# Attention outputs stored as 64 rows and one row, keys stored once and loaded in two pieces

## The chip, the core and the metric

The kernel runs on one core of a Trainium2 chip. The metric is device microseconds of one execution; three executions of the kernel before took 1837.16, 1839.26 and 1840.21 us, and their median, 1839.26 us, is the time before. One more execution was taken with the hardware profiler; all views below are of that one.

A core has a matrix engine (TensorE, PE in the profile; PEld is its weight load), a vector engine (DVE), a scalar engine (ACT), a general engine (POOL) and SyncE (SP), which computes nothing and here issues almost all DMAs. Each engine works through its own list of instructions in order. A DMA is issued by one engine's queue ("SPq" in the views) and then carried out by 16 DMA engines that all queues share.

## The reference, cut to what matters

One layer of gated cross-attention and a gated feed-forward, in float32, on 16 x 128 = 2048 tokens of width 1024:

```python
# x: (16, 128, 1024); ctx_4096: (16, 128, 1024)
def xattn(queries, keys, values, Wq, Wk, Wv, Wo):    # 32 heads of 32, 8 key/value heads, groups of 4
    q = (queries @ Wq).reshape(b, s, KV_HEADS, GROUP, HEAD_DIM)
    k = (keys @ Wk).reshape(b, s, KV_HEADS, HEAD_DIM)
    v = (values @ Wv).reshape(b, s, KV_HEADS, HEAD_DIM)
    scores = jnp.einsum('bqhgd,bkhd->bhgqk', q, k) * scale
    attn = jax.nn.softmax(scores, axis=-1)
    return jnp.einsum('bhgqk,bkhd->bqhgd', attn, v).reshape(b, s, EMBED) @ Wo
def ffn(x, W_gate, W_up, W_down):                     # width 2752
    return silu(x @ W_gate.T) * (x @ W_up.T) @ W_down.T
x = x + jnp.tanh(g_xattn[0]) * xattn(_layernorm(x), ctx_4096, ctx_4096, Wq, Wk, Wv, Wo)
x = x + jnp.tanh(g_ffn[0]) * ffn(_layernorm(x), W_gate, W_up, W_down)
```

Each of the 16 sequences has 128 tokens and attends only to its own 128 context rows, so attention falls into 16 x 8 = 128 independent pieces of 128 keys by 4 x 128 queries.

## The kernel before

**Numbers in two parts.** The matrix engine multiplies in a shortened float32. Every operand is therefore split into a high part (the rounded number) and a low part (the rest), by `split`: a copy on ACT and a subtraction on DVE. A product is three matmuls: high x high, high x low, low x high (`mm3`).

**Stages.** Tokens are handled in two halves of 1024 (`NGRP`), with blocks of 512 (`TB`). `projections` makes keys, values and queries for both halves and sends them to DRAM: `kd`, `vd`, `qd`. `attention` reads them back, piece by piece, and sends outputs to `od`. `outer` reads `od`, multiplies by the output projection, adds the residual and normalizes; `run` then does the feed-forward, with seven products in place of eight.

**Attention is woven into other work.** It is a generator; the host loop takes one step of it at a time between its own matmuls. The first half's attention (called stage 1 here) runs inside the second half's projections, from about 107 to 348 us; the second half's (stage 2) runs inside the feed-forward of the first half, from about 478 to 861 us. The instruction order on each engine is the order in which the Python code issues the work; nothing rearranges it. What DMAs SP issues therefore stand in one list: loads of attention, stores of attention, loads and stores of the host.

**One cell of attention** is one sequence and two key/value heads, so 64 cells, 32 in each stage, and two units in each cell. For a cell, SP issues `vta` (values, L458), `ks` (keys, L451) and `qs` in two pieces (L465, L466). The keys of a cell lie in SBUF on 96 partitions: high part, high part again, low part, 32 rows each, so that one matmul over 96 rows does the three products at once with the queries' high, low, high. For that `kd` holds three parts: `evacuate` (L246 to L255) stores high and low with one DMA into its parts 1 and 2, and the high part with a second DMA into part 0; one DMA (L451) then loads the 96 rows. `ks` has two buffers, and its next load is issued once the second score matmul of its cell is done.

A unit goes through `scores` (PE, L472), `take` (ACT copy, then a maximum over partitions on POOL, L483), `shift` (DVE, L486), `expo` (ACT, L489 and L491), `rest` (DVE, L495), `gather` (PE, L500 and L501) and `leave` (a copy of 80 rows out of PSUM into `os`, L511, on ACT, or in stage 1 in turn on ACT and DVE). Values are padded with 16 columns of ones (`ONES`), so that `gather` gives 64 rows of outputs (with the values' high part and low part) and 16 equal rows that hold the sums of the softmax. `leave` stores all 80 rows to `od` with one DMA (L515). In stage 1 the store is issued a step later, and `os` has three buffers; in stage 2 it is issued at once, and `os` has one buffer, so that the next copy has to wait for the store to land. When a sequence's eight units are stored, the row of sums (row 64, one of the sixteen) is fetched as `rc` (L526), inverted, and kept in `rd`. `outer` reads rows 0 to 31 and 32 to 63 of `od` and the inverted sums of `rd`.

**Semaphores of DMAs.** SP's DMAs take eight semaphores in turn; a DMA is issued only when the one eight before it has landed.

## Time and profile before

| | |
|---|---|
| median of three executions | 1839.26 us (1837.16 to 1840.21) |
| profiled execution | 1839.81 us, span of its instructions 1838.0 us |
| PE | busy 1816.5 us, 99% of the span, 8296 matmuls |
| DVE, ACT, POOL | busy 1210.6, 900.7 and 546.3 us |
| DMA | 373.55 MB in 232565 packets, mean 203 GB/s |
| `od<-os` | 128 DMAs of 160 KB, median 4.0 us from issue to landing |
| `ks<-kd` | 64 DMAs of 96 KB, 4.0 us |
| `kd<-e` | 8 DMAs of 512 KB, 6.7 us, and 8 of 256 KB, 6.8 us |
| `rd<-rc` | 16 DMAs of 16 KB, 2.4 us |

Busy time is the union of an engine's instructions. An entry of the view of waits says which engine stood idle before which instruction, who ended the wait, and for how long in total, how often and at longest. A line `SPq L515 DMA_DIRECT2D od<-os` of the timeline is the issuing of a DMA, with start and duration; the transfer itself goes on after that, until its landing. The chain of waits is followed back from the last instruction: at each step to what released it. "PEclk" is the matrix engine's granted clock as a share of full speed, and the DMA share is the mean busy share of the 16 DMA engines.

### The profile page before, as it was taken

The page shows a single profiled execution, that of the slowest core. Times are in us where ns is not written, and L with a number is a line of the kernel's source. Part 1 is how long each engine was busy: PE and PEld are TensorE (multiplying, and loading weights), DVE is VectorE, ACT ScalarE, POOL GpSimd, SP SyncE. Part 2 cuts the span into 40 slices and gives each one's busy share as a digit, 9 for nine tenths or more (in the row PEclk, how much of TensorE's full clock was granted, in tenths as well). Part 3 has the DMA queues.
Part 4 walks back from the last instruction along what each step waited for, and adds up shares of the span by engine and source line. Part 5 has one row for each costly group of instructions (what it writes and reads, how often), then busy time and mean ns, then how long its engine had stood idle before and what let it go on. Part 6 is the DMA issues. An engine that isn't in the chain of part 4 may idle for free.

```text
span 1838.0 us, 23463 instructions
## 1 busy us (share of the span) xinstructions
PE 1816.5 (99%) x8296; PEld 1493.4 (81%) x8296; DVE 1210.6 (66%) x1551; ACT 900.7 (49%) x1301; POOL 546.3 (30%) x372
## 2 busy tenths in 40 slices
PE   9999999999999999999999999999999999999999
PEld 8877877888877777787888888888888888888887
DVE  6758778668877777776578635355356656745765
ACT  4457787435677777776434434333334212312321
POOL 1136566221233333331021233244330231122021
PEclk9999999999999999999999999999999999999999
DMA  9699999774555455543674565675666566665764
GB/s 331 208 274 289 285 285 269 239 258 134 159 146 151 144 148 146 147 138 118 218 252 161 145 204 187 188 210 168 170 206 258 201 233 204 245 215 180 258 201 157
DMA packets 232565, 373.55 MB, mean 203 GB/s; under 512 B 38016, under 2 KB 124288, under 8 KB 227328
## 3 DMA queue, kind: packets, MB, share of 16 engines
q1 hardware_dynamic: 210400, 333.77, 55.7%
q10 hardware_dynamic: 14112, 25.17, 4.6%
q0 software_dynamic: 7936, 13.11, 4.4%
q8 instruction: 66, 1.08, 0.2%
q14 instruction: 51, 0.42, 0.1%
HBM read 247.99 MB, written 122.42 MB: 202 GB/s over the span
## 4 chain that ended last, share of the span: by engine, by line
PE 85%; DVE 5%; DMA 4%; ACT 2%; issue 2%; POOL 1%; SPq 1%; DVEq 0%; POOLq 0%; ACTq 0%
PE bx L707 36%; PE bz L707 18%; PE by L707 9%; PE bz L124 3%; PE bz L122 3%; PE bz L123 3%; PE bx L124 3%; PE bx L123 3%; PE bx L122 3%; PE av L501 1%; DMA od<-os 1%; PE av L500 1%; DVE pl L495 1%; POOL mx L483 1%; DVE pr L486 1%
## 5 line engine op out<-in xcount | busy, mean ns | idle before, releaser
L483 POOL PARTITION_ALL_REDUCE mx<-pr x128 | 276.1, 2157 | 343.4 <-ACT pr L481 167.3
L674 POOL TENSOR_TENSOR sum<-raw 128x512 f32<-128x512 f32 (+1 forms) x37 | 48.0, 1298 | 479.4 <-DVE stc L115 479.4
L114 ACT CAST sta<-raw 128x1024 fp32r<-128x1024 f32 (+1 forms) x66 | 67.7, 1026 | 241.7 <-PE by L707 232.6
L707 PE MATMUL bz<-m5h,stb 128*128 128x512 f32 (+1 forms) x528 | 169.9, 383 | 0.0
L707 PE MATMUL bx<-m4h,std 128*128 128x512 f32 x512 | 168.8, 390 | 1.0 <-DVE c L753 0.8
L707 PE MATMUL bx<-m6h,stb 128*128 128x512 f32 (+1 forms) x528 | 169.6, 383 | 0.0
L707 PE MATMUL bx<-m7h,stc 128*128 128x512 f32 x512 | 168.6, 389 | 0.0
L707 PE MATMUL bz<-m3h,stc 128*128 128x512 f32 x512 | 168.5, 389 | 0.0
L707 PE MATMUL by<-m2h,sta 128*128 128x512 f32 x512 | 168.5, 389 | 0.0
L707 PE MATMUL bx<-m1h,sta 128*128 128x512 f32 x512 | 168.4, 389 | 0.0
L751 DVE TENSOR_TENSOR c<-by,c 128x512 f32<-128x512 f32 x42 | 28.8, 687 | 144.1 <-issue 137.6
L495 DVE TENSOR_TENSOR pl<-pr,ph 128x512 fp32r<-128x512 f32 x128 | 121.0, 945 | 2.2 <-PE av L501 2.2
L144 POOL TENSOR_TENSOR rs__143<-ve,mhalf 128x1 f32<-128x1 f32 x32 | 29.3, 916 | 312.4 <-DVE nm L142 303.0
L851 DVE SCALAR_TENSOR_TENSOR c<-bx,tg,c 128x512 f32<-128x512 f32 x96 | 72.0, 750 | 66.3 <-PE bx L707 62.5
L707 PEld LDWEIGHTS bz<-m5h,stb 128*128 128x128 f32 x528 | 98.2, 188 | 20.2 <-DVE stb L115 0.5
L707 PEld LDWEIGHTS bx<-m6h,stb 128*128 128x128 f32 x528 | 98.4, 188 | 20.0
L707 PEld LDWEIGHTS bx<-m4h,std 128*128 128x128 f32 x512 | 96.1, 188 | 22.6 <-DVE c L753 1.2
L707 PEld LDWEIGHTS bx<-m7h,stc 128*128 128x128 f32 x512 | 96.1, 188 | 20.5 <-issue 0.2
L707 PEld LDWEIGHTS by<-m2h,sta 128*128 128x128 f32 x512 | 96.1, 188 | 20.5
L707 PEld LDWEIGHTS bx<-m1h,sta 128*128 128x128 f32 x512 | 96.1, 188 | 20.4
L707 PEld LDWEIGHTS bz<-m3h,stc 128*128 128x128 f32 x512 | 96.1, 188 | 20.1
L486 DVE TENSOR_TENSOR pr<-pr,mx 128x512 f32<-128x512 f32 x128 | 87.6, 684 | 37.0 <-POOL mx L483 36.7
(400 smaller groups left out, 4635.9 us busy)
## 6 DMA issues: line engine op xcount, KB each, us to landing
raw<-in_wgu SPq DMA_DIRECT2D x42, 1024.0 KB, 6.7
x1d<-c SPq DMA_DIRECT2D x96, 256.0 KB, 2.8
c<-x1d ACTq DMA_DIRECT2D x96, 256.0 KB, 3.0
hd<-c SPq DMA_DIRECT2D x86, 256.0 KB, 2.2
od<-os SPq DMA_DIRECT2D x128, 160.0 KB, 4.0
qd<-e SPq DMA_DIRECT2D x32, 512.0 KB, 5.5
qs<-qd SPq DMA_DIRECT2D x64, 256.0 KB, 4.4
raw<-od SPq DMA_DIRECT2D x32, 512.0 KB, 5.1
```

What stands on the lines that cost most here:

```text
L114: nc.scalar.copy(h, src)
L122: nc.tensor.matmul(ps, lh, rh, start=first, stop=False)
L123: nc.tensor.matmul(ps, lh, rl, start=False, stop=False)
L124: nc.tensor.matmul(ps, ll, rh, start=False, stop=last)
L144: nc.gpsimd.tensor_tensor(rs, ve, mhalf, ALU.pow)
L483: nc.gpsimd.partition_all_reduce(mx[n], pr[n], P, bass_isa.ReduceOp.max)
L486: nc.vector.tensor_tensor(pr[n], pr[n], mx.pop(n), ALU.subtract)
L495: nc.vector.tensor_tensor(pl[n], pr.pop(n), f32(ph[n]), ALU.subtract)
L674: lambda: tt(s1, a[1][0], a[1][1], sub),
L707: nc.tensor.matmul(ps, l_, r_, start=start and k == i == 0, stop=k == n - 1 and i == 2, skip_group_check=not start)
L751: tt(c[1], ps, c[1], ALU.add)
L851: nc.vector.scalar_tensor_tensor(y, ps, g, y, ALU.mult, ALU.add)
```

## The change

The outputs' store becomes two DMAs: rows 0 to 63, and then row 64 alone. The other 15 rows of sums are still computed and copied out of PSUM, but not stored; `od` has 65 rows in place of 80. The keys' store becomes one DMA, with high and low part; `kd` has two parts in place of three. The keys' load becomes two DMAs: rows 32 to 95 of the tile (high and low) and then rows 0 to 31 (high again). What lies in SBUF is the same as before, and so are all instructions of PE, DVE, ACT and POOL; the lists of waits before some of them name one more DMA semaphore. SP issues 1148 DMAs and other shown instructions in place of 964.

```diff
-        kd[t] = dr.tile([3, HD, KV, TB], F32, name=f"kd{t}")
+        kd[t] = dr.tile([2, HD, KV, TB], F32, name=f"kd{t}")
...
-        od[b] = dr.tile([VW, KV // 2, 2, G, P], F32, name=f"od{b}")
+        od[b] = dr.tile([2 * HD + 1, KV // 2, 2, G, P], F32, name=f"od{b}")
...
                         z = kd[2 * g + a][:, ts(f, HD // 2)]
-                        evacuate(acc[f], z[1:3], z[0:1])
+                        evacuate(acc[f], z)
...
                 h = slice(2 * c, 2 * c + 2)
-                nc.sync.dma_start(f32(ks[m]), kd[t].rearrange("s d h t -> (s d) h t")[:, h, bt])
+                nc.sync.dma_start(f32(ks[m][HD:]), kd[t].rearrange("s d h t -> (s d) h t")[:, h, bt])
+                nc.sync.dma_start(f32(ks[m][:HD]), kd[t][0][:, h, bt])
...
             def store():
-                nc.sync.dma_start(od[bb][:, k % 4, k // 4], os_)
+                for z in (slice(0, 2 * HD), slice(2 * HD, 2 * HD + 1)):
+                    nc.sync.dma_start(od[bb][z, k % 4, k // 4], os_[z])
```

## The prediction

> **What bounds the kernel now.** I read the page first, then PE's idle time by stretch, then who ends PE's waits there, then the chain of waits, and last SP's list of issues. The page:

> ```profile
> PE 1816.5 (99%) x8296; PEld 1493.4 (81%) x8296; DVE 1210.6 (66%) x1551; ACT 900.7 (49%) x1301; POOL 546.3 (30%) x372
> ```

> PE is the bound. The change gives PE no work and takes none, so it can win only PE's idle time and can lose only by making more of it. Idle PE, from busy time by stretch (PE, PEld, DVE, ACT, POOL, then clock, DMA share, GB/s):

> ```profile
> 165.00:215.00 50.00, 46.37 (x271) 38.76 (x271) 41.10 (x63) 37.15 (x68) 31.21 (x15) 1.00 0.98 286
> 215.00:335.00 120.00, 116.92 (x550) 93.60 (x549) 92.33 (x130) 94.38 (x160) 74.72 (x34) 0.99 0.91 265
> 480.00:870.00 390.00, 385.88 (x1679) 309.09 (x1678) 293.01 (x365) 297.98 (x452) 134.00 (x64) 1.00 0.50 144
> 280.00:284.00 4.00, 4.00 (x11) 3.13 (x12) 2.32 (x5) 2.69 (x5) 2.49 (x2) 0.57 0.91 253
> ```

> Idle are 3.63 us, 3.08 us and 4.12 us; the rest of attention (100 to 165, 335 to 480) has under 0.7 us. At 280 to 284 us the clock was 0.57, a loss of 4 x 0.43 = 1.7 us behind a stall. So what the change can reach in stage 1 is 3.63 + 3.08 + 1.7 = 8.4 us, and in stage 2 4.1 us. Who ends PE's waits in these (first 165 to 215, second 215 to 335, third 480 to 870):

> ```profile
> PE by L472 <- DMA qs<-qd: 1.2, 2, 0.9
> ...
> PE av L500 <- DVE os L511: 2.4, 1, 2.4
> ...
> PE av L501 <- DVE pl L495: 3.0, 4, 1.2
> ```

> Behind these the chain of waits has DMAs (start, length):

> ```profile
> 182.27 4.43 DMA od<-os
> 203.01 7.32 DMA od<-os
> ...
> 272.84 3.72 DMA raw<-in_wo
> ...
> 652.35 4.38 DMA od<-os
> 675.22 3.59 DMA od<-os
> ```

> A store of outputs that lands late keeps the buffer of `os`, its next copy waits, and ACT or DVE waits with it. SP's issues from 193 us on:

> ```profile
> 193.30 0.94 SPq L253 DMA_DIRECT2D kd<-e  x2
> 194.28 1.53 SPq L515 DMA_DIRECT2D od<-os  x1
> 195.90 1.11 SPq L458 DMA_DIRECT2D vta<-vd  x1
> 197.11 0.75 SPq L451 DMA_DIRECT2D ks<-kd  x1
> 197.91 1.67 SPq L465 DMA_DIRECT2D qs<-qd  x1
> 199.64 0.62 SPq L466 DMA_DIRECT2D qs<-qd  x1
> ```

> No gap stands between them: SP is late here. After the two stores of keys the next issues take 1.53, 1.11 and 1.67 us, against a median of 0.41 for `od<-os` and a least of 0.53 for that `qs`: SP is held back while the DMA engines, 0.98 busy, drain. So in stage 1 SP's list and the DMA engines are both nearly full, and the change loads the one and relieves the other.

> **The change part by part.**

> *Keys stored once.* Eight DMAs of 256 KB go, at 0.45 us of issue (median of `kd<-e`) and 262 KB / 286 GB/s = 0.92 us of all DMA engines each. Four stand at 22 to 37 us, where ACT waited 6.3 us for one to land, but PE was idle only 0.15 us: I take -0.1. Four stand at 176 to 202 us and relieve that stretch by 4 x 0.50 = 2.0 us of SP (with a 0.05 us step between issues) and 3.7 us of DMA.

> *Keys loaded twice.* 64 more issues, 32 in each stage, at 0.32 (least of `ks<-kd`) to 0.62 us (the 32-row `qs`); I take its own median 0.42, plus 0.05: 0.47. Bytes stay. Queued behind it on SP are both `qs` loads and the next `od` store; the score matmul waits for `qs`, and a fourth semaphore for PE's queue costs 0.02 us by the chain's rows, hidden under a 0.23 us matmul.

> *Outputs stored twice.* 128 more issues. The nearest row is the 16 KB `rd<-rc`, least 0.32 us; the median of `od<-os` is 0.41. I take 0.32 + 0.05 = 0.37. Each pair moves 30 KB less, 31 KB / 286 GB/s = 0.11 us. `os` is free when both have landed: the second is issued 0.37 us later but its nearest row lands in 1.4 us at best (`rd<-rc`) against 1.9 for `od<-os`, and under load it lands just behind the first in the same queues. So 0 to +0.37 us later; I take +0.1.

> [...]

> *Sum for SP.* A cell gets 0.47 + 2 x 0.37 = 1.21 us more. One cell at 286.6 to 294.0 us has 6.1 us of issues in 7.35 us, of which 1.6 us is such holding back (0.95 and 1.47 in place of 0.4): 4.5 us of its own. After: 5.7 to 7.3 of 7.35 us. It fits, barely.

> *165 to 215 us.* The stretch has 14 output stores and 7 key loads: SP gets 14 x 0.37 + 7 x 0.47 - 2.0 = +6.5 us; the DMA engines get 3.7 + 14 x 0.11 = 5.2 us less, and SP's long issues should shrink by about as much. The two nearly cancel; the late store at 203 us stands right behind two key stores. I take -0.5; bounds -3.6 (all stalls gone) and +3.6 (doubled).

> *215 to 335 us.* 17 cells: SP +17 x 1.21 = 20.6 us, DMA 34 x 0.11 = 3.7 us less, no key stores. The big stall (2.4 us, then the clock's 1.7) hangs on two loads of `in_wo` in series, each issued by SP when DVE freed its buffer, with 0.8 us of SP slack ahead of them: each lands 0 to 0.5 us later. I take +0.6, and +0.3 for `qs` landing later elsewhere; bounds -4.8 (3.08 and 1.7 gone) and +4.

> [...]

> *Stage 2.* SP has room (DMA share 0.50), but `os` has one buffer. ACT waited 19.0 us, 14 times, for `od<-os` to land. Where the store was ready early but stood in SP's list behind other work, as at 652.35 us behind `ks` (650.60) and two `qs`, it now stands behind one more issue: +0.47, and +0.1 for the pair. What is late next is `pl` on DVE and the second matmul of `gather`: PE's weight load waited 10 times for it, 7.6 us. I take four of these pushed by the full 0.57 us: +2.3. Bounds 0 and 10 x (0.47 + 0.37) = +8.4.

> *After 870 us* `outer` reads the same 64 rows: 0.

> Sum: -0.1 - 0.5 + 0.6 + 0.3 + 2.3 = +2.6 us. On the profiled 1839.81 that is 1842.4; it was 0.55 us over the median of the runs, so I forecast **1841.9 us**.

> **The rivals.**

> *SP's list becomes the bound in stage 1.* For: from 169 to 207 us SP already has next to no gap, and PE loses 3.63 in 50 us, 7%. Should that state spread to 215 to 335 us, PE loses 120 x 0.073 = 8.7 in place of 3.1 us, +5.6; the first stretch doubles, +3.6; two more drops of the clock, +3.4; stage 2 +2.3: +15, 1854 us. Against: a third of SP's time there is holding back by the DMA engines, which shrinks. It decides where a cell's issues exceed about 6.9 us, the distance of two cells' score matmuls in the chain (292.53 and 299.45 us); my range of 5.7 to 7.3 includes that.

> *The DMA engines were the bound, and their relief wins.* For: share 0.98 and 0.91, SP held back after each pair of key stores. Stage 1 moves 4 x 262 KB + 64 x 31 KB = 3.0 MB less, 10.5 us of DMA engines. Half of the reachable 8.4 us goes, mostly the 280 us stall and its clock, and stage 2 stays: -4.2, 1835 us. Against: PE is 97% busy there, and the stall of 280 us hangs on DVE's order too. It decides where that stall falls under about 2 us and the clock holds.

> *Nothing reaches PE.* The waits on `pl` and `qs` have slack elsewhere, SP catches up: 1839.3 us. Against: 10 waits on `pl` have none.

> **How the numbers follow.** What a measurement of this kernel tells from no change is about 0.2%, 3.7 us. The forecast gets 0.42, with its own range 1837 to 1847; SP-bound 0.22; relief 0.20; nothing 0.16. Of the forecast's 0.42 a little under half lies beyond +3.7 us (0.19), of nothing 0.02, and all of SP-bound: slower 0.43. Of relief 0.16 and of the others 0.02 lie beyond -3.7 us: faster 0.18. Within: 0.39. The range 1834 to 1852 holds the forecast, nothing, nearly all of relief and the lower half of SP-bound.

> **What would show it.** Right: `os` waits on `od<-os` of 20 to 28 us in stage 2, PE idle 5 to 7 us there; the issues behind `kd<-e` shorter than 1.1 us; 165 to 215 us within 1 us of 3.6. SP-bound: SP's issues without gaps from 215 to 300 us, `qs<-qd` ending many more of PE's waits, the clock under 1 in more stretches. Relief: landings of `od<-os` in 165 to 215 us well under 5.6 us (median), and a full clock at 280 us. I am wrong if a one-row store costs SP far more than 0.4 us or lands far later than its 64 rows, or if a stall of under 2 us brings the clock down.

## The result, and the profile after

The changed kernel takes 1868.15 us (median of four executions, 1865.11 to 1871.49), the kernel before beside it 1838.83 us (1837.16 to 1840.21): a ratio of 1.0156, with a 95% interval of 1.0142 to 1.0171. It is 29 us slower; the forecast was 1841.9 us and its range ended at 1852. The profiled execution took 1869.55 us, its span is 1867.7 us.

The page's line of the engines:

```profile
PE 1825.3 (98%) x8296; PEld 1495.6 (80%) x8296; DVE 1209.6 (65%) x1551; ACT 899.2 (48%) x1301; POOL 536.3 (29%) x372
```

PE, DVE, ACT and POOL run the same instructions as before; SP issues 1150 DMAs by the trace, 966 before. But PE is idle longer (42.4 us in place of 21.5). Where, shows the view by stretch (length; PE, PEld, DVE, ACT, POOL; granted clock, DMA share, GB/s):

```profile
100.00:165.00 65.00, 61.61 (x267) 48.50 (x266) 43.77 (x54) 46.14 (x74) 32.46 (x15) 1.00 0.87 257
165.00:215.00 50.00, 44.70 (x239) 36.59 (x238) 36.05 (x54) 32.92 (x59) 27.00 (x14) 0.97 0.87 249
215.00:335.00 120.00, 106.22 (x503) 83.99 (x502) 81.36 (x119) 80.94 (x141) 59.99 (x30) 0.96 0.82 233
480.00:870.00 390.00, 383.52 (x1668) 306.92 (x1667) 295.98 (x367) 294.30 (x446) 131.72 (x67) 1.00 0.51 142
```

PE's idle time in these four is 3.4, 5.3, 13.8 and 6.5 us, against 0.1, 3.6, 3.1 and 4.1 us before. Most of the loss is in stage 1, and most of that from 215 us on, where the keys' stores are over (the last is issued at 210.5 us). The DMA engines are *less* busy than before (0.82 against 0.91), so nothing says that they are what is short. Who ends PE's waits from 100 to 335 us (sum, times, longest), and the first three entries:

```profile
PE by L473 <- DMA qs<-qd: 12.9, 8, 3.2
PE by L473 <- ACT ph L492: 4.1, 2, 2.2
PE by L473 <- DMA od<-os: 2.2, 2, 1.7
```

The score matmul now waits for its queries; before, that entry had 1.2 us. The chain of waits says why they are late (start, length, what):

```profile
281.12 8.16 DMA qd<-e
...
289.30 0.32 SPq L452
...
289.67 0.57 SPq L466
...
290.29 0.63 SPq L467
...
291.01 0.54 SPq L262
...
291.65 6.49 DMA qd<-e
...
298.16 0.58 SPq L466
...
298.79 0.63 SPq L467
...
300.16 6.67 DMA qd<-e
...
306.85 0.31 SPq L452
```

No computing engine's work is in this loop. A 512 KB store of queries (`qd<-e`) holds one of the eight semaphores for 6.49 to 8.16 us; the DMA eight places later in SP's list was issued 0.02 us after the landing in all three turns (landed at 289.28, 298.14 and 306.83 us, issued at 289.30, 298.16 and 306.85); behind that stand the queries' loads and soon the next `qd<-e`. The trace of before, which has the landings of all of SP's 966 DMAs, shows the same: they name eight semaphores (98 DMAs of ACT's queue share them), and each of the 958 that take one again was issued after the DMA before on it had landed, 23 of them within 17 ns of that. SP's list over one turn of the loop (start, duration):

```profile
291.65 0.41 SPq L253 DMA_DIRECT2D qd<-e  x1
292.19 2.93 SPq L517 DMA_DIRECT2D od<-os  x4
295.22 0.38 SPq L459 DMA_DIRECT2D vta<-vd  x1
295.69 0.62 SPq L451 DMA_DIRECT2D ks<-kd  x1
296.94 0.32 SPq L452 DMA_DIRECT2D ks<-kd  x1
298.16 0.58 SPq L466 DMA_DIRECT2D qs<-qd  x1
```

The load at 298.16 us is the eighth DMA behind `qd<-e`, and the gap ahead of the last is the wait for the store's landing at 298.14 us (291.65 + 6.49). Without the two one-row stores and the second key load, five DMAs would stand here and not eight, and the eighth would be tried that much later; this last is argued from the list, and the experiments below test it. The two turns here take 8.5 and 9.1 us (289.67, 298.16 and 307.21 us, the first pieces of the queries' loads); before, two cells' scores lay 6.9 us apart.

This loop is one stretch of stage 1. In the whole of it, from 127 to 358 us, SP waited 32.4 us for the DMA eight before, and only 8.4 us of that for `qd<-e`; 19.8 us were for the host's loads of weights and inputs (`raw`, mostly 512 KB each).

The stalls also cost the clock: it was halved (0.5) for 3.4 us from 179, 251, 295 and 312 us and, in stage 2, from 865 us, each time 0.01 to 1.02 us behind a stall of 1.48 to 3.19 us; before, once in these stages, from 280.5 us, 0.6 us behind one of 2.36 us. One of these, by stretch:

```profile
294.00:299.00 5.00, 3.72 (x9) 2.70 (x10) 3.32 (x7) 1.61 (x3) 2.08 (x1) 0.66 0.76 267
```

**The ledger.** Between the first scores of stage 1 and its last lie 243.3 us, 22.7 more than before: in the three stretches 15.7 us more idle time (22.5 against 6.8), 0.9 us more behind them (335 to 480 us), and three more drops of 1.7 us, together 21.7. Between the first and last scores of stage 2 lie 371.0 us, 4.5 more: 2.4 us of idle time and 1.7 of the drop. What follows stage 2 took 2.3 us more, which no step of the change explains and which lies within what other runs below show there (991 to 998 us). Stage 2's 4.5 us are no surer: three runs below whose stage 2 is that of the changed kernel took 367.4 to 368.3 us there, and one whose stage 2 is that of the kernel before took 370.6.

### The profile page after: what moved, and what is told of

It reads as the page before. It is cut to its first block, busy times and chain, and to the rows that moved or that the text cites. A ratio compares the mean times of both kernels' runs of the same rounds, so it can differ in the third digit from the quotient of the medians.

```text
span 1867.7 us, 23684 instructions
## 1 busy us (share of the span) xinstructions
PE 1825.3 (98%) x8296; PEld 1495.6 (80%) x8296; DVE 1209.6 (65%) x1551; ACT 899.2 (48%) x1301; POOL 536.3 (29%) x372
## 4 chain that ended last, share of the span: by engine, by line
PE 77%; DMA 10%; DVE 4%; ACT 3%; SPq 3%; issue 2%; POOL 1%; ACTq 0%; DVEq 0%; POOLq 0%
PE bx L709 34%; PE bz L709 17%; PE by L709 9%; DMA od<-os 3%; PE bx L124 3%; PE bz L124 3%; PE bx L123 3%; PE bz L123 3%; PE bz L122 3%; PE bx L122 2%; DMA qd<-e 2%; PE av L502 1%; POOL mx L484 1%; PE av L501 1%; DMA raw<-in_wqkv 1%
## 5 line engine op out<-in xcount | busy, mean ns | idle before, releaser
L484 POOL PARTITION_ALL_REDUCE mx<-pr x128 | 265.2, 2072 | 381.3 <-ACT pr L482 166.0
L496 DVE TENSOR_TENSOR pl<-pr,ph 128x512 fp32r<-128x512 f32 x128 | 116.0, 906 | 5.7 <-ACT pr L490 2.5
L709 PEld LDWEIGHTS bx<-m4h,std 128*128 128x128 f32 x512 | 96.1, 188 | 22.5 <-DVE c L853 1.2
L115 DVE TENSOR_TENSOR stb<-sum,stb 128x1024 fp32r<-128x1024 f32 (+1 forms) x66 | 79.4, 1204 | 48.2 <-ACT stb L114 48.2
```

Of the source, the lines that this page charges most:

```text
L115: nc.vector.tensor_tensor(l, src, f32(h), ALU.subtract)
L484: nc.gpsimd.partition_all_reduce(mx[n], pr[n], P, bass_isa.ReduceOp.max)
L496: nc.vector.tensor_tensor(pl[n], pr.pop(n), f32(ph[n]), ALU.subtract)
L709: nc.tensor.matmul(ps, l_, r_, start=start and k == i == 0, stop=k == n - 1 and i == 2, skip_group_check=not start)
```

## The experiments

All times by ratio to the kernel before beside them; "+10 us" is the ratio's excess on 1839 us. Two such differences can be told apart when they lie more than about 4 us apart, by their intervals; stage lengths below are of the one profiled execution of each run. In the expectations, theory A is that SP's list is overfull in stage 1: by the issues' own time (A1), or with it by the wait for the DMA eight before (A2). Theory B is that the second store of a pair holds `os` too long.

| run | time, us | ratio, 95% interval | us |
|---|---|---|---|
| the change | 1868.15 | 1.0156 (1.0142 to 1.0171) | +28.7 |
| keys only | 1851.87 | 1.0081 (1.0065 to 1.0098) | +14.9 |
| outputs only | 1850.97 | 1.0075 (1.0059 to 1.0091) | +13.8 |
| 65 rows in one DMA | 1838.11 | 0.9998 (0.9985 to 1.0010) | -0.4 |
| change, row stores on POOL | 1852.47 | 1.0085 (1.0070 to 1.0100) | +15.6 |
| change, 16 query stores on POOL | 1856.22 | 1.0088 (1.0071 to 1.0106) | +16.2 |
| change, 16 row stores on POOL | 1863.68 | 1.0125 (1.0106 to 1.0143) | +23.0 |
| keys, stage 2 only | 1849.49 | 1.0055 (1.0034 to 1.0076) | +10.1 |
| before, query stores on POOL | 1840.53 | 0.9996 (0.9984 to 1.0008) | -0.7 |
| keys by head, 96 rows | 1845.29 | 1.0026 (1.0010 to 1.0042) | +4.8 |
| all in pieces of 96 and 80 rows | 1866.36 | 1.0143 (1.0128 to 1.0157) | +26.3 |
| keys in stage 2, store first | 1839.08 | 0.9991 (0.9980 to 1.0003) | -1.7 |
| before, store first | 1837.80 | 0.9991 (0.9980 to 1.0002) | -1.7 |
| change, store first | 1864.96 | 1.0137 (1.0123 to 1.0151) | +25.2 |
| the same, row stores of stage 1 on POOL | 1844.43 | 1.0023 (1.0011 to 1.0034) | +4.2 |
| 16 query stores on POOL, 16 short ones on SP | 1861.84 | 1.0118 (1.0101 to 1.0136) | +21.7 |
| before, 65 rows, store first | 1836.44 | 0.9983 (0.9974 to 0.9993) | -3.1 |

**1. Each half of the change alone.** The first leaves the outputs as before, the second the keys.

```diff
+                nc.sync.dma_start(f32(ks[m][HD:]), kd[t].rearrange("s d h t -> (s d) h t")[:, h, bt])
+                nc.sync.dma_start(f32(ks[m][:HD]), kd[t][0][:, h, bt])
```

> Only the keys' part of the change: kd stored once, ks loaded in two pieces; outputs stored as before with one DMA of 80 rows. Theory A, SP's list (time to issue, and waiting for the DMA eight before to land): stage 1 gets 32 issues more and 4 fewer, some 16 of the 40 us of issuing that the whole change adds, so about 40% of its +29 us: 1851 us, with scores waiting for qs. Theory B, the buffer of os is held by the second, one-row store: this run has none, so 1839 us. Theory C, the DMA engines: 1 to 2 us faster than before, since four key stores of 256 KB are gone from stage 1.

```diff
+                for z in (slice(0, 2 * HD), slice(2 * HD, 2 * HD + 1)):
+                    nc.sync.dma_start(od[bb][z, k % 4, k // 4], os_[z])
```

> Only the outputs' part: od stored as 64 rows and one row, keys as before (stored twice, loaded once). Theory A: 64 issues more in stage 1 at 0.45 us, 28 of 40 us, 60 to 70% of the loss: 1857 us. Theory B: nearly the whole loss, 1866 us, with ACT and DVE waiting for od to land far longer than the 28 us of before. If the two parts only add up, this run and the keys alone make +29 us together; if a full list is what counts, each alone costs less than its share, and the two together less than 29.

+14.9 and +13.8 us: the two totals come to the whole, 28.7. But they lose it in different places. Outputs only: stage 1 took 227.0 us from first to last scores (220.6 before), stage 2 366.0 (366.5). Keys only: stage 1 223.0, stage 2 373.0. So stage by stage they do not add up: in stage 1 the halves lost 6.4 and 2.4 us and the whole change 22.7, far more than both; in stage 2 the keys alone lost 6.5 and the whole change 4.5. That the totals agree is a coincidence.

**2. The bytes without the second DMA.**

```diff
+                nc.sync.dma_start(od[bb][:, k % 4, k // 4], os_[: 2 * HD + 1])
```

> The bytes alone: outputs stored with one DMA of 65 rows in place of 80, keys as before. As many issues as before, 30 KB less for each store. Theory A: no loss, 1836 to 1840 us. Theory C: a gain of 1 to 3 us if the DMA engines held stage 1. If 65 rows land much later than 80 (65 is no multiple of 16), os is held longer: up to +5 us.

Fifteen of sixteen rows of sums less, in one DMA, is worth 0.4 us with an interval around nothing. So the bytes saved are worth nothing that can be measured, and the loss is all in the splitting. ACT waited 16.3 us for `os` in stage 2 (19.0 before), so nothing shows 65 rows to hold the buffer longer than 80.

**3. The second store, but not on SP.**

```diff
+                for eng, z in ((nc.sync, slice(0, 2 * HD)), (nc.gpsimd, slice(2 * HD, 2 * HD + 1))):
+                    eng.dma_start(od[bb][z, k % 4, k // 4], os_[z])
```

> The changed kernel, but the 128 one-row stores are issued by POOL's queue: they leave SP's list and its eight semaphores, while the buffer of os is still held until the one row has landed. Theory A: as the keys alone, about 1851 us. Theory B: as the whole change or worse, 1866 to 1872 us. POOL's maximum (2.1 us a unit, 3.4 us apart) may be pushed by its issues: up to +5 us on either.

`os` still waits for two DMAs, and the time falls to that of the keys alone. Stage 1 took 223.7 us, 19.6 less than in the change; stage 2 took 376.0, 5.0 more. So theory B falls, and the outputs' part of the loss in stage 1 comes from one more DMA of each pair in SP's list.

**4. Long landings or many issues.** The change, with the stores of the second half's queries issued by POOL (16 by the trace, 12 of them before stage 1's last scores; the expectations speak of 15); then, in place of that, with 16 of the one-row stores issued by POOL; then the first of these on the kernel before.

```diff
-                evacuate(ps, qd[2 * g + a][f // 2, :, ts(f % 2, HD // 2)])
+                evacuate(ps, qd[2 * g + a][f // 2, :, ts(f % 2, HD // 2)], eng=nc.gpsimd if g else nc.sync)
```

> The changed kernel, but the 512 KB stores of queries that stand in stage 1 (15 of the 16 of the second half) are issued by POOL. That takes 15 issues at 0.43 us, 6 to 7 us, out of SP's list, and 15 long transfers (6.5 to 8 us to land) out of the eight semaphores. Theory A1, SP's time to issue is what counts: a sixth of the added 41 us of issuing goes, so 4 to 5 us of the +29 come back: 1863 us. Theory A2, the wait for the DMA eight before counts, as the chain of the changed kernel has it, where qd's landing releases the next issue again and again from 281 to 307 us: 10 to 16 us come back, 1852 to 1858 us. POOL's issues take 1.3 us each by its other DMAs and can cost its maximum up to 3 us.

```diff
+                row = nc.gpsimd if gap == 1 and n % 4 == 1 else nc.sync
+                for eng, z in ((nc.sync, slice(0, 2 * HD)), (row, slice(2 * HD, 2 * HD + 1))):
+                    eng.dma_start(od[bb][z, k % 4, k // 4], os_[z])
```

> The changed kernel, but 16 of stage 1's 64 one-row stores (every fourth) are issued by POOL: as many issues out of SP's list as with the queries on POOL, and about as long ones (0.44 us), but short transfers out of the semaphores. Theory A1: the same 4 to 5 us back as with the queries on POOL, 1863 us. Theory A2: less than half of what the queries on POOL give back, 1862 to 1868 us.

> The kernel before with the same 15 stores of queries issued by POOL: a relief of SP's list and of the semaphores where nothing was added. Theory A1 and A2: stage 1 of the kernel before still has 5 to 6 us of idle PE behind late qs, od and in_wo; 0 to 4 us of that come back, 1835 to 1839 us. If POOL's extra 15 x 1.3 us of issuing matter: up to 3 us slower.

The long DMAs off SP's list bring back 12.5 us, 16 short ones 5.7 us; on the kernel before, the same long ones bring nothing. So before, SP's list had room for them. In stage 1 itself, which took 243.3 us in the change, the two runs took 234.4 and 240.7 us: 8.9 and 2.6 us less. The rest of what they won lies behind stage 1, most of it in stage 2 and after it, where nothing was changed. A short DMA thus cost between 0.16 us (2.6 / 16) and 0.36 us (5.7 / 16), and a long one more. The next run holds the number of issues fixed: where POOL takes a query store, SP gets a store of one row, 2 KB, to memory that nobody reads.

```diff
+                if few is not None:
+                    nc.sync.dma_start(few, f32(e[:1, 0]))
```

> The whole change with the 15 query stores of stage 1 on POOL, as in the run that took 1856.2 us, and in the place of each on SP a store of one row, 2 KB, to memory that nobody reads. SP issues as many DMAs as in the whole change, but none of these 15 holds its semaphore for 6 to 8 us. If the number of issues decides, the time goes back to 1864 us or more. If the long landing eight DMAs back decides, it stays at 1856 to 1859 us. By the 5.7 us that 16 one-row stores were worth, both at once would be 1861 to 1863 us.

+21.7 us: by the ratios the short ones cost 5.5 us, and 7.0 us of the change's 28.7 went with the long landings. The trace does not bear out the second part. Stage 1 took 244.7 us, no less than the change's 243.3, its scores again waited for `qs<-qd` (12.3 us from 100 to 335 us, 12.9 in the change), and PE's idle time is as long as there, 2.3, 7.6 and 12.4 us in the three stretches; the last two:

```profile
165.00:215.00 50.00, 42.41 (x215) 34.37 (x214) 34.79 (x52) 30.82 (x55) 22.72 (x12) 0.93 0.80 233
215.00:335.00 120.00, 107.56 (x526) 85.37 (x525) 82.69 (x121) 83.03 (x145) 69.11 (x41) 0.97 0.81 240
```

SP still waited 30.7 us for the DMA eight before, 22.3 of it for the host's loads. What this run had less of lies behind stage 1, most of it in stage 2 and after it, where both kernels issue the same. So the short DMAs put back brought all of the loss in stage 1 back (234.4 to 244.7 us): that the number of DMAs in the list acts is shown. Whether the long landings of the query stores add to it stays open: the two runs that took DMAs out say that they do, this one says that they don't.

**5. Does a piece's own issue time matter?** In stage 2, where SP is not pressed, the trace has the bare price. SP's issues of the keys and outputs there, first the kernel before (count: least/median/greatest ns):

```profile
L451 SPq DMA_DIRECT2D ks<-kd x30: 317/354/1972, 484.9 to 825.1; - x30
L515 SPq DMA_DIRECT2D od<-os x64: 303/322/1482, 499.2 to 862.3; - x64
```

then after the change (64 rows of keys, 32 rows of keys, both pieces of the outputs):

```profile
L451 SPq DMA_DIRECT2D ks<-kd x32: 587/616/1917, 496.0 to 850.1; - x32
L452 SPq DMA_DIRECT2D ks<-kd x32: 583/585/1340, 496.7 to 852.1; - x32
L517 SPq DMA_DIRECT2D od<-os x122: 430/452/1206, 523.0 to 876.6; - x122
```

Here a piece takes longer to issue than the whole did (part of that is not its shape but that it follows another DMA at once, 0.58 against 0.32 us for the 32 rows; see the last section). Keys cost 0.616 + 0.585 - 0.354 = 0.85 us more for a cell, outputs 2 x (2 x 0.452 - 0.322) = 1.16 us. Two runs split into as many pieces, but of all 96 and all 80 rows: the keys by head, and then the outputs by halves of their columns too.

```diff
+                for z in range(2):
+                    nc.sync.dma_start(f32(ks[m][:, z]), kd[t].rearrange("s d h t -> (s d) h t")[:, 2 * c + z, bt])
...
+                for z in (slice(0, 2), slice(2, 4)):
+                    nc.sync.dma_start(od[bb][:, k % 4, k // 4, z], os_[:, z])
```

> The kernel before, with only this: each cell's keys, still stored in three parts, are loaded in two DMAs of 96 rows, one for each head. As many issues and semaphores as with the split into 64 and 32 rows, but with 96 rows each, a shape that took 0.35 us to issue in stage 2 where the pieces of 64 and 32 rows took 0.58 to 0.62. Theory 'time of issue': a cell's keys cost SP about 2 x 0.35 = 0.70 us in place of 0.35, +0.35 to +0.4 against +0.85 of the split into 64 and 32 rows, so under half of that run's +13 us: 1843 to 1846 us. Theory 'number of DMAs' (the wait for the DMA eight before): as the split into 64 and 32 rows, 1850 to 1853 us.

> As the keys by head, and the outputs also stored in two DMAs, each of all 80 rows and half the columns. The number of DMAs is that of the whole change, 320 in stage 1, but each has 80 or 96 rows; bytes are those of the kernel before. Theory 'time of issue': a cell costs SP about 0.4 + 2 x 0.33 = 1.06 us more in place of 2.0, half of it: 1846 to 1856 us. Theory 'number of DMAs': as the whole change, 1865 to 1870 us, or a little more for the bytes.

The first answers as the time of issue would: +4.8 us against +14.9. The second doesn't: +26.3 us, nearly all of the change's loss. Its expectation rested on 0.33 us for a piece, and that failed: the pieces' issues, keys of the first run, then keys and outputs of the second, were

```profile
L452 SPq DMA_DIRECT2D ks<-kd x60: 303/416/1094, 485.5 to 829.0; - x60
```

```profile
L452 SPq DMA_DIRECT2D ks<-kd x64: 303/417/1381, 498.2 to 852.5; - x64
L517 SPq DMA_DIRECT2D od<-os x123: 303/422/767, 524.7 to 879.3; - x123
```

so a cell cost 0.48 + 1.04 = 1.52 us more, three quarters of the change's 2.01 and not half. The loss in stage 1 was 21.3 us, as in the change (22.7), with the same sign, PE's waits from 100 to 335 us:

```profile
PE by L473 <- DMA qs<-qd: 16.0, 11, 2.9
```

So a shape that is cheaper to issue in stage 2 wins next to nothing in stage 1. There the 326 DMAs of this run took 177.6 us to issue and the change's 320 took 174.5, the same for each, so the run does not separate the price from the waits; what the two lists share is the number of DMAs. What goes with the loss over the runs is SP's slack. From 20 us after stage 1's first scores to 8 us after its last, I added up how long SP stood waiting for other engines' work (its slack) and for the DMA eight before:

| run | SP's DMAs | slack, us | wait for the DMA eight before, us | first to last scores, us |
|---|---|---|---|---|
| before | 242 | 64.7 | 15.1 | 220.6 |
| keys only | 265 | 47.2 | 13.6 | 223.0 |
| keys by head | 269 | 42.7 | 17.2 | 220.7 |
| store first, row stores on POOL | 265 | 43.2 | 12.1 | 223.5 |
| outputs only | 300 | 30.3 | 20.8 | 227.0 |
| change, queries on POOL | 311 | 27.2 | 21.4 | 234.4 |
| change, 16 row stores on POOL | 308 | 28.2 | 25.4 | 240.7 |
| 96 and 80 rows | 326 | 23.5 | 27.8 | 241.9 |
| the change | 320 | 21.9 | 32.4 | 243.3 |
| queries on POOL, 16 short ones on SP | 323 | 23.6 | 30.7 | 244.7 |

About 25 more DMAs cost stage 1 between nothing and 3 us; from there on the loss grows steeply while the slack hardly falls any further and the wait for the DMA eight before grows. That is one trace of each kernel, and goes together; it doesn't show which of the two drives the other. The sum of the issues' own time doesn't sort these runs: it was 174.5 us in the change but also 169.3 us in the run with row stores on POOL, where the DMA engines were busier (0.90 to 0.95 against 0.82 to 0.87); that this made its issues longer is likely and not shown.

**6. The keys' part, in stage 2.** Keys stored once and loaded twice for the second half alone, first as they are, then with the loads of keys and queries issued at the end of the step, behind `leave`'s store of the outputs; then that same move on the kernel before.

```diff
+                if gap == 1:
+                    nc.sync.dma_start(f32(ks[m]), kd[t].rearrange("s d h t -> (s d) h t")[:, h, bt])
+                else:
+                    nc.sync.dma_start(f32(ks[m][HD:]), kd[t].rearrange("s d h t -> (s d) h t")[:, h, bt])
+                    nc.sync.dma_start(f32(ks[m][:HD]), kd[t][0][:, h, bt])
```

> The keys' part in stage 2 alone: the third and fourth block of 512 tokens are stored once and loaded in two pieces, the first two as before; outputs as before. In the keys alone, stage 2 was 6.5 us longer than before (373.0 in place of 366.5 us from its first to its last score matmul) and stage 1 only 2.4 us. If that is the split loads: 1844 to 1846 us, with ACT waiting about 33 us for od to land. If it is the lateness that stage 2 takes over from stage 1, or chance: 1838 to 1841 us.

```diff
-                load_k(m + 2)
                 qs.pop(m)
-                load_q(m + nq)
+                loads = lambda: (load_k(m + 2), load_q(m + nq))
+                if gap == 1:
+                    loads()
+                else:
+                    behind.append(loads)
...
+            while behind:
+                behind.pop(0)()
             yield
```

> Keys stored once and loaded in two pieces in stage 2 alone (+10 us by itself, 1849.5), but with the loads of keys and queries of stage 2 issued at the end of the step, behind the outputs' store and not ahead of it. If the outputs' store stands late in SP's list behind the slow key issues, and ACT's copy waits for the one buffer: +10 falls to between -1 and +3 us, 1838 to 1843 us, and ACT's waits for the outputs' buffer in stage 2 fall from 31 to 20 us or less. If the keys' loss in stage 2 is their own landing or PE's longer list of waits: no gain, 1848 us or more.

> The kernel before with only the same move: in stage 2 the loads of keys and queries are issued behind the outputs' store. If the store's place in SP's list is what ACT waits for, ACT's 19 us of waits for the outputs' buffer fall to 12 or less, and of PE's 4.1 us of idle time in stage 2 up to 3 go: 1836 to 1838.5 us. If those waits are the transfer itself: 1838.5 to 1840 us. If the later loads are missed by the score matmuls: 1841 us or more.

The move takes the whole +10.1 us away, and a little more. ACT's wait for the one buffer of `os` in stage 2 (us, times, longest), with the keys as they are and then with the move:

```profile
ACT os L515 <- DMA od<-os: 30.8, 14, 3.9
```

```profile
ACT os L519 <- DMA od<-os: 2.4, 2, 1.2
```

Before the change it was 19.0 us, 14 times. The order in SP's list is what differs; first the run with the keys as they are, then the start of the same place with the move:

```profile
652.36 0.58 SPq L454 DMA_DIRECT2D ks<-kd  x1
652.99 0.59 SPq L455 DMA_DIRECT2D ks<-kd  x1
653.62 0.54 SPq L469 DMA_DIRECT2D qs<-qd  x1
654.21 0.63 SPq L470 DMA_DIRECT2D qs<-qd  x1
654.93 0.54 SPq L519 DMA_DIRECT2D od<-os  x1
```

```profile
651.75 0.39 SPq L523 DMA_DIRECT2D od<-os  x1
652.25 0.58 SPq L455 DMA_DIRECT2D ks<-kd  x1
```

Four issues, 2.6 us with the steps, stand right ahead of the store that frees `os`; with the move the store goes first. Stage 2 took 374.9 us without the move and 364.4 with it, and 364.4 as well when the kernel before got the same move. So it is shown that the key loads hurt stage 2 by delaying another DMA in the list, and not by their own landing or by PE's longer list of waits, both of which the move leaves as they are. On the kernel before, the move cut the same waits to 1.1 us, but the gain of 1.7 us is inside its interval: there PE rarely waited for them.

**7. Do the causes add up?** The whole change with the store first, and then with the 64 one-row stores of stage 1 on POOL as well.

> The whole change, with stage 2's loads of keys and queries issued behind the outputs' store. If stage 2's part of the loss is the store's place in SP's list, and stage 1's part is independent of it, what falls is stage 2's excess in the whole change (371.0 us from its first to its last scores, against 366.5 before) and the about 2 us that the same move won on the kernel before: 4 to 8 us, 1860 to 1864 us. If the second, one-row store holds the single buffer anyway: under 2 us, 1866 us or more.

```diff
+                row = nc.gpsimd if gap == 1 else nc.sync
+                for eng, z in ((nc.sync, slice(0, 2 * HD)), (row, slice(2 * HD, 2 * HD + 1))):
+                    eng.dma_start(od[bb][z, k % 4, k // 4], os_[z])
```

> As the run before it, and the 64 one-row stores of stage 1 are issued by POOL and not by SP. If the loss is stage 1's overfull list on SP and stage 2's order, and nothing else, only the split key loads of stage 1 are left (stage 1 took 2.4 us more with the keys alone, and most runs of it lie within 4 us of before): 1838 to 1844 us. If something else of the change costs too: 1847 us or more.

The first brings 3.5 us, a little under the 4 to 8 expected, and that is inside the two intervals; its stage 2 took 367.2 us, as it did without the move in the runs of part 4 (367.4 to 368.3). So for the whole change it isn't shown that the order cost stage 2 anything. The second brings 21.0 us more, which is 0.33 us for each of the 64 stores, and it is stage 1 that wins them: 243.9 us falls to 223.5. Of 28.7 us, 4.2 are left, with the stretches from 100 us on

```profile
100.00:165.00 65.00, 63.45 (x276) 50.37 (x275) 44.24 (x54) 45.07 (x72) 35.60 (x24) 1.00 0.95 269
165.00:215.00 50.00, 46.65 (x268) 39.02 (x267) 39.98 (x60) 36.05 (x66) 34.06 (x28) 1.00 0.95 268
215.00:335.00 120.00, 114.99 (x547) 90.49 (x546) 92.97 (x133) 93.12 (x160) 84.76 (x67) 1.00 0.90 256
```

that is 9.9 us idle in stage 1 against 6.8 before. Stage 1 is as long as with the keys alone (223.0), so what is left goes with the keys' 32 more issues there. The clock held in all three.

One thing stays open: in the profiled executions stage 2 took 8.4 us more with the keys of stage 2 alone, 6.5 with the keys alone and 9.5 with all row stores on POOL, but 4.5 in the whole change and 0.9 to 1.8 in the three runs of part 4 with the same stage 2, whose lists there are longer. ACT waited less for `os` in the whole change (23.9 us) than with the keys of stage 2 alone (30.8). Why was not tried.

**8. A version faster than both.** The kernel before, with 65 rows in one DMA and stage 2's loads behind the outputs' store.

> The kernel before with the outputs stored as 65 rows in one DMA and stage 2's loads issued behind the outputs' store; keys as before. If the two small gains add: 1836 to 1838 us, an interval wholly below before. If they are nothing: 1838.5 to 1840.5 us.

1836.44 us, 0.9983 of before, and the interval (0.9974 to 0.9993) excludes no change: 3.1 us, where each part by itself could not be told from nothing.

## Why the prediction was wrong

It named the right mechanism as a rival, "SP's list becomes the bound in stage 1", and gave it 0.22 and 1854 us. The signs that it listed for this rival came true: `qs<-qd` ended 12.9 us of PE's waits in place of 1.2, and the clock dropped in four places of stage 1 and not in one. The forecast itself failed in these steps:

- **215 to 335 us: "+0.6, and +0.3", bounds -4.8 and +4.** This is the term of the sum that failed most: +10.7 us idle and two more drops, 3.4, so +14.1. I let the list's extra issues come to nothing but loads landing a little later, because I took it that SP would still fit. In its place the runs showed SP's list to be the limit of stage 1: with 64 one-row stores off it, stage 1 fell from 243.9 to 223.5 us. The bounds came from the stalls seen before, and those bound nothing once SP's list becomes the limit. I had also left 100 to 165 us at nothing, "under 0.7 us" being idle: +3.3 us. (The "17 cells" are a little high too: the trace of before has 15 key loads and 35 output stores there, 20.0 us by my prices and not 20.6.)
- **The price of an issue: "0.47" for the second key load, "0.37" for the one-row store.** I priced the added piece alone and left the other at the whole's price. By the medians of stage 2 a cell got 0.85 + 1.16 = 2.01 us, where I had 1.21, or 1.06 without the steps between issues. The price alone is not the whole of it: with 1.52 us a cell the loss was nearly the same (+26.3). (The wait of one semaphore more in PE's own queue took 0.05 us in the trace of before, 281 times, where I had 0.02 from rows of other queues; no term used it.)
- **"After: 5.7 to 7.3 of 7.35 us. It fits, barely."** With 2.01 us it is 6.5 to 8.1 us, most of it above the point of about 6.9 us that the text itself gave. And the count put a wait at nothing, without a reason: a list that is nearly full reaches the DMA eight places on before a 512 KB store or load has landed (6.49 to 8.16 us for the stores in the loop shown). The front part of this document tells of the eight semaphores, and the trace of before had a 512 KB store of keys, values or queries among most cells' DMAs; I didn't put the two together. SP's wait for the DMA eight before rose from 15.1 to 32.4 us. From 215 to 335 us alone, SP spent 75.1 us issuing before and 89.8 after, of 120; its waits for other engines fell from 40.2 to 8.9 us, and those for the DMA eight before rose from 6.3 to 18.3. So time of issue, which is all that I counted, did not fill the list.
- **165 to 215 us: "-0.5; bounds -3.6 and +3.6".** Idle time +1.7 us and a drop of the clock, 1.7: +3.4, inside the bounds. Most issues behind `kd<-e` did get shorter (0.4 to 0.8 us, one of 2.06), but that did not make up for the issues added. That busy DMA engines hold SP back was my estimate: in the trace of before 32 of the 36 issues of over 0.9 us fell where those engines were over 0.7 busy, but so did 509 shorter ones.
- **The rival's +15, 1854 us.** Its price came from the worst stretch before (7% idle). From 215 to 335 us PE was idle 11.5% of the time, with more drops than the two that I allowed.
- **Stage 2: "+2.3", bounds 0 and +8.4.** +4.5 in the profiled execution, +0.9 to +1.8 in three others with the same stage 2, so this term did not fail. The signs named came true: ACT waited 23.9 us for `os` (20 to 28 said), PE was idle 6.5 us (5 to 7 said). Keys alone lost more there, and for the keys of stage 2 alone the cause is shown to be the one that the text named, the store standing behind `ks` and `qs`.
- **Right:** the early key stores are worth nothing (stage 1 began 0.4 us earlier); the bytes are worth nothing (65 rows in one DMA: 0.9998); the pair's release of `os` costs nothing to be seen ("+0.1"; row stores on POOL, still in pairs, lost no more than the keys alone). The DMA engines of the rival that was given 0.20 were indeed less busy, 0.82 against 0.91 from 215 us on, and won nothing that can be seen.

I had said that I would be wrong "if a one-row store costs SP far more than 0.4 us ... or if a stall of under 2 us brings the clock down". The pieces took 0.45 us, little more than that; the second came true (below). The landings of `od<-os`, which I also named as a sign, can't be read: the profile of the changed kernel shows no landing times for these DMAs.

I weighed the splits only by bytes, landing and the added piece's issue. Here each of 64 one-row stores on SP's pressed list cost 0.33 us of the whole kernel's time (21.0 us in all).

## What to carry to other kernels

Before splitting a DMA, count what its queue has left: the waits of the issuing engine for *other engines* are its slack. Here, once they had shrunk from 65 to about 25 us of stage 1, each short DMA more cost about a third of a microsecond at the end, whatever bytes it saved. Price both pieces of a split and not the added one only, and look at which DMA is so many places back as there are semaphores (here eight): in the loop shown, a store there that took 6.49 to 8.16 us to land turned a short list into a wait. Where a buffer has one copy, issue the DMA that frees it ahead of loads that have time; that undid all of the loss, 10.1 us, when only stage 2's keys were split and, with the smaller store, won 0.17% on the kernel before.
